# Shared blocks: the last products of a step are placed behind the first products of the next step

## The chip, the cores and the metric

The kernel runs on one core of one Trainium2 chip. The metric is the device time of one execution in microseconds. Three runs of the kernel before the change took 1549.39, 1553.00 and 1556.89 us; the median is 1553.0 us. The profile is of a further execution, and the sums below are made against that one.

## What is computed

The reference passes 2048 tokens of 256 channels (`x`, 2 x 1024 x 256, fp32) through four layers. Each layer adds to `x` what a conditioning stage followed by a mixture-of-experts stage makes of it. Cut to what this change touches:

```python
# layer 0, after its conditioning (32 routed experts, one per token)
shared = (silu(h @ shared_gate_w) * (h @ shared_up_w)) @ shared_down_w     # 256 -> 512 -> 256
x = x + shared + routed
# layer 2, conditioning: 2 shared experts of width 512, stacked to one of width 1024, and 8 routed, top 2
# layer 2, ffn: 8 shared experts of width 128, stacked to one of width 1024, and 8 routed, top 2
# layer 3, conditioning: one shared expert of width 512, and 8 routed, top 2
# layer 3, ffn: 16 experts with a capacity of 160 tokens each (no shared expert)
```

The shared part is the same computation in all four places: two products with the tokens, a silu and a multiplication, and a product back to 256 channels. Layer 1 has no shared expert.

## The kernel before

**The tiling.** Tokens are worked in four blocks of 512 (`TB`), the hidden width in pieces of 128. One call of `_shared` (L1347) does one block of tokens: it runs over `nf` pieces of the hidden width, 4 in layers 0 and 3 and 8 in the two stages of layer 2. One turn of that loop is called a step here. There are 16 steps in layer 0, 32 in the conditioning of layer 2, 32 in its ffn stage and 16 in layer 3: 96 steps.

**A step.** TensorE makes the first products `spg` and `spu` (L1360), each a sum over two halves of the 256 channels, in two PSUM tiles of the tag "mm", of which there are four. ScalarE makes `ssg = silu(spg)` (L1365), VectorE makes `sa = ssg * spu` (L1367), and TensorE makes the last products from `sa`: four matmuls (L1370), one for each 128 tokens of the block, which add into the two PSUM tiles `spo`. In the trace each of these fp32 matmuls has two records, so a step has four of `spg`, four of `spu` and eight of `spo`. After the last step of a block, VectorE or ScalarE adds or copies `spo` into the token-major arrays (L395, L1760, L1859). `ssg` and `sa` have two buffers each.

**What sets the order.** The program is written as a list, and a planner in the compiler orders each engine's queue from it at compile time: by the order in the list, by the dependences, and by its own estimate of when each input is ready. It may pull later work forward while an earlier instruction is not ready by that estimate. `_behind` (L1329) adds an edge that only fixes an order on one engine's queue; it makes nothing wait on a semaphore. On the chip each queue is worked in the order planned.

**What hangs on a step.** `_shared` takes two callbacks. `mid(f, mul, mm)` is called after the first products; `hook(f, mul, mm)` is called after the last products; `mul` is the multiplication of a step and `mm` the last matmul. Through them other work is spread over the steps:

- In the stages that lead (three blocks of tokens in each of the two conditioning stages and the layer 2 ffn stage), `Lead.hook` (L317) starts the routing at the 2nd and 4th step (1st and 3rd in layer 3), and then sends token rows to DRAM with `Rows.scatter` (L278), an indirect DMA from GpSimd: two for each step in layer 2, four in layer 3, each made to wait for that step's `mul`. The routed slots that follow load these rows (`xs<-xbuf`, L297, SyncE), and a load waits for all 32 sends.
- In the stages that close (the last block of tokens), `Tokens.hook` (L1468) is both `hook` and `mid`: it loads routed outputs (`yt<-tbuf`), adds them on VectorE behind `mul` (L1459), and transposes finished tokens on TensorE behind `mm` (`_back`, L1378). In layer 3 it also starts pieces of the last stage (`Last.at`, L1963).
- In layer 0, the first two blocks have no callback; the last two gather routed outputs (`Combine.hook`, L1408), and the loads of layer 1's weights wait for the first step's `mul` (L631).

In time, the program is: layer 0 with its first two blocks (53 to 103 us), its routed slots, its last two blocks (279 to 327 us), layer 1, and then for each of the three further stages a lead, the routed slots and a closing block; the layer 3 ffn stage ends it.

Of the kernel before, what the change touches and what calls it, by code (L numbers as in the profile page):

```python
# [19 lines left out]
P = 128  # L20
# [281 lines left out]
class Lead:  # L302
# [14 lines left out]
    def hook(self, f, mul, mm):  # L317
        self.n += 1
        if self.n in self.at:
            self.part()  # L320
            if not self.at:

                for _ in range(min(self.per, len(self.sends))):
                    self.sends.pop(0)()
        elif self.n > self.late:
            for _ in range(min(self.per, len(self.sends))):
                self.sends.pop(0)(mul)
# [56 lines left out]
def _layer0(k):  # L384
# [6 lines left out]
    def shared(tb, hook=None):  # L391
        po = _shared(k, pool, psum, HT, tb, *shw, hook)
        for i in range(2):
            t = tb * 4 + i * 2
            nc.vector.tensor_tensor(Xt[:, t:t + 2, :], po[i], Xt[:, t:t + 2, :], ALU.add)  # L395
# [933 lines left out]
def _behind(k, inst, ref):  # L1329

    k.tc.add_manual_dep(inst.ins, ref.ins.name,
                        mybir.DependencyInfo(mybir.DependencyClass.NoSync,
                                             mybir.DependencyReason.SCHED_ONLY))
# [13 lines left out]
def _shared(k, pool, psum, X, tb, W1, W3, W2, nf, hook=None, mid=None):  # L1347

    nc = k.nc
    cols = slice(tb * TB, (tb + 1) * TB)
    po = [psum.tile([P, 2, D], F32, name="spo%d" % i, tag="o", bufs=2) for i in range(2)]
    mul = None
    for f in range(nf):
        pg = psum.tile([P, TB], F32, name="spg", tag="mm")
        pu = psum.tile([P, TB], F32, name="spu", tag="mm")
        for ps, W in ((pg, W1), (pu, W3)):
            for c in range(2):
                mm = nc.tensor.matmul(ps, W[:, c, f * P:(f + 1) * P], X[:, c, cols],  # L1360
                                      start=c == 0, stop=c == 1)
        if mid:
            mid(f, mul, mm)
        sg = pool.tile([P, TB], F32, name="ssg", tag="sg")
        k.silu = nc.scalar.activation(sg, pg, AF.Silu)  # L1365
        a = pool.tile([P, TB], F32, name="sa")
        mul = nc.vector.tensor_mul(a, sg, pu)  # L1367
        for g in range(4):

            mm = nc.tensor.matmul(po[g // 2][:, g % 2, :], a[:, g * P:(g + 1) * P], W2[:, f, :],  # L1370
                                  start=f == 0 and g % 2 == 0, stop=f == nf - 1,
                                  skip_group_check=True)
        if hook:
            hook(f, mul, mm)
    return po


# [263 lines left out]
class Split:  # L1641
# [32 lines left out]
    def end(self, i, aT, cols):  # L1674
        n, nc = self.n, self.k.nc
        po = self.psum.tile([P, D], F32, name="fpo", tag="o", bufs=2)
        self.stage([nc.tensor.matmul(po[r, :], aT[:, f, r], w[2][:, f, :], start=f == 0,
                                     stop=f == n - 1, skip_group_check=True)
                    for f in range(n) for r, w in cols])
        y = self.pool.tile([P, D], F32, name="ys", bufs=4)  # L1680
        nc.scalar.copy(y, po)
        self.slots.put(i, y)
# [21 lines left out]
def _cond_moe(k, name, wr, bias, W1, W3, W2, nf, hold, R1, R2, gate_mult, final, lead, next=None):  # L1704
# [47 lines left out]
    def shared(tb, hook=None, mid=None, added=lambda: False):  # L1752
        po = _shared(k, pool, psum, XT, tb, W1, W3, W2, nf, hook, mid)
        for i in range(2):
            t = tb * 4 + i * 2
            if added():
                nc.vector.scalar_tensor_tensor(Ht[:, t:t + 2, :], po[i], final, Ht[:, t:t + 2, :],
                                               ALU.mult, ALU.add)
            else:
                nc.scalar.activation(Ht[:, t:t + 2, :], po[i], AF.Copy, scale=final)  # L1760
# [51 lines left out]
def _layer2_ffn(k):  # L1812
# [42 lines left out]
    def shared(tb, hook=None, mid=None):  # L1855
        po = _shared(k, pool, psum, HT, tb, *shw, hook, mid)
        for i in range(2):
            t = tb * 4 + i * 2
            nc.vector.scalar_tensor_tensor(Xt[:, t:t + 2, :], po[i], 1.0 / 16.0, Xt[:, t:t + 2, :],  # L1859
                                           ALU.mult, ALU.add)  # L1860
# [510 lines left out]
```

## Time and profile before

| | |
|---|---|
| runs before, median of 3 (lowest to highest) | 1553.0 us (1549.39 to 1556.89) |
| the profiled execution | 1554.72 us |
| its span, first to last instruction | 1553.0 us, so 1.7 us lie around it |
| mean granted TensorE clock | 0.977 |
| TensorE busy / VectorE / ScalarE / GpSimd | 95% / 31% / 20% / 18% |
| first products, L1360, four groups | 102.1 + 97.5 + 91.6 + 90.4 us busy |
| last products, L1370 | 192.5 us busy in 768 records |
| DMA | 252.43 MB in packets, 163 GB/s mean |

A matmul's busy time runs to its modelled end, and matmuls overlap: a 512-column matmul of `spg` has a mean of about 600 ns though the next one follows 430 ns later. So the distance between starts says what a matmul costs in a full queue, and the busy column doesn't. "PEld" is the weight load, which overlaps the matmul before it. "Idle before" is time in which the engine had nothing running ahead of an instruction of the group, with what ended it.

### The profile page before, as it was taken

What the parts mean: (1) busy time and instruction counts of PE and PEld (TensorE: products, weight loads), DVE (VectorE), ACT (ScalarE), POOL (GpSimd) and SP (SyncE); (2) the same over time, 40 slices, a digit from 0 to 9 for tenths busy, and PEclk for the clock granted to TensorE, in tenths of its full rate; (3) what the DMA queues carried; (4) which work ended last, traced back from release to release, by engine and by line L of the source; (5) the groups of instructions that cost most, each with busy time, mean ns of one, the idle gap of its engine ahead of it and who ended that gap; (6) DMA issues with size and microseconds to landing.
All of it is one profiled execution on the core that took longest, in us unless ns stands there. A gap on an engine that the chain in (4) does not pass through costs nothing. (4 is left out here: it accounts for less than half of the span.)

```text
span 1553.0 us, 23694 instructions
## 1 busy us (share of the span) xinstructions
PE 1470.2 (95%) x8649; PEld 1021.0 (66%) x8652; DVE 478.2 (31%) x1596; ACT 303.9 (20%) x642; POOL 285.2 (18%) x317
## 2 busy tenths in 40 slices
PE   6989999999999999999999999999999989998897
PEld 2543333444555886555699999999985547864675
DVE  3732222324411444421111111111114414446432
ACT  2311212123111212211111111111111212126222
POOL 0400000300331441033001001010010253420342
PEclk9989999999999999999999999999999999999799
DMA  9859995923211684051053254155517437762470
GB/s 253 273 201 332 337 352 175 255 72 123 96 48 35 195 252 136 0 214 52 28 185 116 94 190 174 36 184 184 180 34 263 139 122 246 214 218 83 146 250 19
DMA packets 184239, 252.43 MB, mean 163 GB/s; under 512 B 17111, under 2 KB 137823, under 8 KB 184112
## 3 DMA queue, kind: packets, MB, share of 16 engines
q1 hardware_dynamic: 164448, 210.92, 42.2%
q0 software_dynamic: 14176, 36.63, 6.6%
q10 hardware_dynamic: 5488, 3.25, 0.7%
q8 instruction: 72, 1.18, 0.3%
q14 instruction: 55, 0.45, 0.1%
HBM read 284.86 MB, written 50.76 MB: 216 GB/s over the span
## 5 line engine op out<-in xcount | busy, mean ns | idle before, releaser
L1370 PE MATMUL spo<-ring,sa 128*128 128x256 f32 x768 | 192.5, 393 | 20.2 <-DVE sa L1367 15.1
L1370 PEld LDWEIGHTS spo<-ring,sa 128*128 128x128 f32 x768 | 140.7, 192 | 101.9 <-DVE sa L1367 71.5
L281 POOL DMA_INDIRECT tbuf<-ys,sdst x114 | 112.1, 984 | 509.4 <-ACT ys L1635 381.9
L1367 DVE TENSOR_TENSOR sa<-ssg,spu 128x512 f32<-128x512 f32 x96 | 65.8, 686 | 327.3 <-PE spu L1360 287.3
L1628 DVE TENSOR_TENSOR fa<-fsg,fpu 128x512 f32<-128x512 f32 x72 | 49.5, 687 | 316.0 <-PE fpu L1623 316.0
L1623 PE MATMUL fpu<-xsT,ring 128*128 128x128 f32 x1152 | 140.4, 275 | 0.0
L1623 PE MATMUL fpg<-xsT,ring 128*128 128x128 f32 x1152 | 140.3, 275 | 0.0
L1623 PEld LDWEIGHTS fpg<-xsT,ring 128*128 128x128 f32 x1152 | 137.1, 192 | 1.9
L1623 PEld LDWEIGHTS fpu<-xsT,ring 128*128 128x128 f32 x1152 | 134.4, 192 | 0.0
L1632 PE MATMUL fpo<-ring,fa 128*128 128x256 f32 x576 | 130.3, 379 | 0.0
L1365 ACT ACTIVATE ssg<-spg 128x512 f32<-128x512 f32 x96 | 57.3, 597 | 347.7 <-PE spg L1360 217.5
L1632 PEld LDWEIGHTS fpo<-ring,fa 128*128 128x128 f32 x576 | 106.7, 190 | 13.0
L1360 PE MATMUL spg<-HT,ring 128*128 128x512 f32 x192 | 102.1, 621 | 5.4 <-issue 2.8
L1360 PE MATMUL spg<-XT,ring 128*128 128x512 f32 x192 | 97.5, 599 | 0.1
L1360 PE MATMUL spu<-HT,ring 128*128 128x512 f32 x192 | 91.6, 596 | 0.0
L1360 PE MATMUL spu<-XT,ring 128*128 128x512 f32 x192 | 90.4, 592 | 0.0
L1599 PE MATMUL cph<-xsT,ring 128*128 128x128 f32 x624 | 83.9, 277 | 6.7 <-DMA ring<-in_L_r 3.7
L1599 PEld LDWEIGHTS cph<-xsT,ring 128*128 128x128 f32 x624 | 76.0, 192 | 10.4 <-DVE sn L1527 4.8
L1606 PE MATMUL cpo<-ring,ch 128*128 128x256 f32 x312 | 80.1, 380 | 0.8 <-ACT ch L1602 0.8
L1627 ACT ACTIVATE fsg<-fpg 128x512 f32<-128x512 f32 x72 | 43.0, 597 | 169.7 <-PE fpg L1623 169.7
L1360 PEld LDWEIGHTS spu<-XT,ring 128*128 128x128 f32 x192 | 36.6, 191 | 43.8 <-issue 43.6
L1360 PEld LDWEIGHTS spu<-HT,ring 128*128 128x128 f32 x192 | 36.6, 194 | 41.9 <-issue 41.7
(574 smaller groups left out, 1656.5 us busy)
## 6 DMA issues: line engine op xcount, KB each, us to landing
ring<-in_L_w SPq DMA_DIRECT2D x108, 1024.0 KB
ring<-in_L_r SPq DMA_DIRECT2D x96, 512.0 KB
ring<-in_L_r SPq DMA_DIRECT2D x156, 256.0 KB
xs<-xbuf SPq DMA_DIRECT2D x138, 129.0 KB
ring<-in_L_W SPq DMA_DIRECT2D x32, 512.0 KB
yt<-tbuf SPq DMA_DIRECT2D x48, 256.0 KB
xbuf<-ACC SPq DMA_DIRECT2D x1, 6063.0 KB
ring<-in_L_s SPq DMA_DIRECT2D x6, 512.0 KB
```

Source lines behind the costliest of these rows:

```text
L281: i = k.nc.gpsimd.indirect_dma_start(out=self.ap, out_offset=bass.IndirectOffsetOnAxis(ap=idx, axis=0), in_=rows, in_offset=None, **end)
L1360: mm = nc.tensor.matmul(ps, W[:, c, f * P:(f + 1) * P], X[:, c, cols], start=c == 0, stop=c == 1)
L1365: k.silu = nc.scalar.activation(sg, pg, AF.Silu)
L1367: mul = nc.vector.tensor_mul(a, sg, pu)
L1370: mm = nc.tensor.matmul(po[g // 2][:, g % 2, :], a[:, g * P:(g + 1) * P], W2[:, f, :], start=f == 0 and g % 2 == 0, stop=f == nf - 1, skip ...
L1599: made = [nc.tensor.matmul(ph[:, f, :], R1[:, c, f * P:(f + 1) * P], xT[:, c, :], start=c == 0, stop=c == 1) for f in range(2) for c in ra ...
L1606: made = [nc.tensor.matmul(po, h[:, f, :], R2[:, f, :], start=f == 0, stop=f == 1) for f in range(2)]
L1623: made = [nc.tensor.matmul(ps[:, j, :], W[:, c, (f0 + j) * P:(f0 + j + 1) * P], xT[:, c, :], start=c == 0, stop=c == 1) for ps, W in ((pg, ...
L1627: nc.scalar.activation(sg, pg, AF.Silu)
L1628: nc.vector.tensor_mul(a[:, f0:f0 + 4, :], sg, pu)
L1632: made = [nc.tensor.matmul(po, a[:, f, :], W2[:, f, :], start=f == 0, stop=f == 4 * nh - 1) for f in range(4 * nh)]
```

## The change

The last products of a step are no longer written after its multiplication. They are kept as a function `end`, and written one step later, after the first products of the next step, with an order edge behind the last of these (`mm`, the last matmul of `spu`). The callback `hook` moves with them, and is called with the old step's `f` and `mul`, and the last matmul of its last products. The last step of a block has no next one: its last products are written at the end without an edge. `mid` stays where it was. No computation, tile, buffer or transfer is added or removed.

```diff
+    def end(f, a, mul, ref):
+        for g in range(4):
+            mm = nc.tensor.matmul(po[g // 2][:, g % 2, :], a[:, g * P:(g + 1) * P], W2[:, f, :],
+                                  start=f == 0 and g % 2 == 0, stop=f == nf - 1,
+                                  skip_group_check=True)
+            if ref is not None:
+                _behind(k, mm, ref)
+        if hook:
+            hook(f, mul, mm)
+
+    old = None
     for f in range(nf):
...
         sg = pool.tile([P, TB], F32, name="ssg", tag="sg")
         k.silu = nc.scalar.activation(sg, pg, AF.Silu)
+        if old:
+            end(*old, mm)
         a = pool.tile([P, TB], F32, name="sa")
         mul = nc.vector.tensor_mul(a, sg, pu)
-        for g in range(4):
-
-            mm = nc.tensor.matmul(po[g // 2][:, g % 2, :], a[:, g * P:(g + 1) * P], W2[:, f, :],
-                                  start=f == 0 and g % 2 == 0, stop=f == nf - 1,
-                                  skip_group_check=True)
-        if hook:
-            hook(f, mul, mm)
+        old = f, a, mul
+    end(*old, None)
     return po
```

## Prediction

> **What bounds the kernel now.** I read the page first: the busy row of TensorE, and the groups of a step.
>
> ```profile
> PE 1470.2 (95%) x8649; PEld 1021.0 (66%) x8652; DVE 478.2 (31%) x1596; ACT 303.9 (20%) x642; POOL 285.2 (18%) x317
> L1370 PE MATMUL spo<-ring,sa 128*128 128x256 f32 x768 | 192.5, 393 | 20.2 <-DVE sa L1367 15.1
> L1370 PEld LDWEIGHTS spo<-ring,sa 128*128 128x128 f32 x768 | 140.7, 192 | 101.9 <-DVE sa L1367 71.5
> ```
>
> TensorE is the bound. The one wait that recurs on it is for `sa` before the last products. How much it costs depends on the row. The first says 20.2 us idle before L1370. The Trainium skill (Perfetto Trace Analysis, section Identifying the Most-Contended Engine) says that matmul busy time is a poor measure of headroom, since pipelined matmuls hide it. So I went to the timeline of one regular step of the layer 2 lead, engine by engine (start, duration, engine, line).
>
> ```profile
> 425.97 0.19 PEld L1360 LDWEIGHTS spg<-XT,ring 128*128 128x128 f32 x1 [0.24 <-issue]
> 426.40 0.19 PEld L1360 LDWEIGHTS spg<-XT,ring 128*128 128x128 f32 x1 [0.24 <-issue]
> 427.41 1.59 PEld L1370 LDWEIGHTS spo<-ring,sa 128*128 128x128 f32 x8 [0.82 <-DVE sa L1367]
> ...
> 426.40 1.02 PE L1360 MATMUL spg<-XT,ring 128*128 128x512 f32 x2
> 427.41 1.99 PE L1370 MATMUL spo<-ring,sa 128*128 128x256 f32 x8
> 429.24 0.59 PE L1360 MATMUL spg<-XT,ring 128*128 128x512 f32 x1
> ...
> 426.67 0.69 DVE L1367 TENSOR_TENSOR sa<-ssg,spu 128x512 f32<-128x512 f32 x1 [4.73 <-PE spu L1360]
> ```
>
> The planner already pulls half of the next `spg` (two records at 426.40) ahead of the last products. That covers 0.86 us of the roughly 1.3 us from the last `spu` to the end of `sa`, not all. First products start 0.43 us apart (425.97, 426.40), so the last products could start at 426.40 + 2 x 0.43 = 427.26; they start at 427.41, when `sa` is done: **0.15 us**. Their first weight load has waited too, so the eight take 427.41 to 429.24 = 1.83 us. Where `sa` is early they take less:
>
> ```profile
> 619.65 1.89 PE L1370 MATMUL spo<-ring,sa 128*128 128x256 f32 x8
> 621.38 1.02 PE L1360 MATMUL spg<-XT,ring 128*128 128x512 f32 x2
> ```
>
> That is 1.73 us, so **0.10 us** more. A full step without waiting is 8 x 0.43 + 1.73 = 5.16 us; the regular one has 5.42 us (427.41 to 432.83). The loss is 0.26 us a step, although the rows above show a TensorE that is "busy" throughout.
>
> I made this subtraction from the start times of all 96 steps. Regular stalls of 0.26 us: 55 steps, 14.2 us. All stalls, by stage: layer 0's first blocks 7.7, its last blocks 5.3, layer 2 conditioning lead 6.6 and close 0.8, ffn lead 7.3 and close 1.0, layer 3 lead 10.8 and close 3.4: **43 us**. By the idle column it would be 20. I take the starts.
>
> **What the change does to it, part by part.** The order becomes g1 u1 o0 g2 u2 o1 (g, u first products, o last products). Between u and its own o now stand the whole g and u of the next step, 3.43 us, instead of 0.86: 2.57 us more cover. Instructions, semaphores and bytes are unchanged; the edge waits for nothing. ScalarE and VectorE keep their work. Banks: u of step f+1 needs the "mm" tile that `sa` of f-1 frees, some 7 us before; `sa` of f+1 needs the buffer that o of f-1 reads, which stands ahead of g and u of f+1. So no new wait there in a regular step. At the end of a block o of the last step now has o of the step before as cover (1.73 us).
>
> - Regular stalls: all go, 14.2 us.
> - Layer 0, first blocks, 7.7 us. One step waits 4.2 us for `sa`, which VectorE had queued behind a comparison of the mask that waits for its load. 4.2 - 2.57 = 1.6 us stays, and 1.6 us of the first two steps isn't a wait for `sa`. Gain 4.5.
> - Layer 0, last blocks, 5.3 us: stalls of 1.5, 1.4 and 1.0 us, where `sa` stands behind gathered rows on VectorE. All under 2.57, so all go. Gain 5.3.
> - Layer 2: 6.6 + 7.3 in the leads (the longest is 1.1 us, behind the routing's burst on VectorE), 0.8 + 1.0 in the closes. Their scatters go out two a step and end some four steps before the lead does, so the slots start with TensorE. Gain 15.7.
> - Layer 3, lead, 10.8 us. Here something else is late next. The scatters:
>
> ```profile
> 1231.86 1.13 POOL L281 DMA_INDIRECT xbuf<-Xt,l3c_rows  x1 [72.36 <-DVE l3c_rows_w L250]
> 1279.17 0.96 POOL L281 DMA_INDIRECT xbuf<-Xt,l3c_rows  x1 [0.30 <-issue]
> 1282.83 1.86 SPq L297 DMA_DIRECT2D xs<-xbuf  x4
> 1286.26 0.41 DVE L1523 COPY xsT<-ps_cm 128x256 f32<-128x256 f32 x1
> 1287.83 1.05 PE L1599 MATMUL cph<-xsT,ring 128*128 128x128 f32 x8
> ```
>
> First scatter 1231.86, last 1279.17, row loads 1282.83, transposed rows 1286.67, first slot 1287.83. The slack is only 1.1 us. In between, GpSimd needs 32 x (0.96 + 0.30) = 40.3 us of the 48.3 from first start to last end: 8 us are its waits for late `sa`. Now the routing is moved as well: `hook` comes one step later, so the logits wait for o0 behind g1 and u1. They began 5.9 us after the stage did; now 2 x 3.43 + 1.73 = 8.6. Its second part stood in the list behind o2, and was pulled ahead of it while `sa` was late; now o2 is ready, and g3 u3 stand in front. I take 3.6 us later in all. GpSimd then runs nearly unbroken, and its end comes 8.0 - 3.6 = 4.4 us earlier; with the slack, 5.5 us at best of the 10.8. TensorE is done some 6 us before the rows are there.
>  That gap is where a rule speaks against the change. The window table (us, busy times, then PEclk, DMA share, GB/s) has:
>
> ```profile
> 86.50:92.30 5.80, 5.80 (x11) 3.87 (x12) 2.34 (x3) 0.28 (x1) 0.00 (x0) 0.50 1.08 372
> ```
>
> After the 4.2 us stall of layer 0 the clock was 0.50 for 5.8 us, a loss of 2.9. The Trainium skill (TensorE: Matmul & The Clock Gate, HAM oscillation) says that an idle window of 3.4 us halves the clock, until a busy one releases it: 1.7 us by the rule for one window, 2.9 by the row. I take the row for the new gap: 5.5 - 2.5 = gain **3**; bounds -3 (the routing slips two steps) and +10.8 (nothing is late).
> - Layer 3, close, 3.4 us. The chain of waits runs there through VectorE and the `yt` loads, not only TensorE:
>
> ```profile
> 1399.08 7.00 DMA yt<-tbuf
> ```
>
> These loads wait for buffers that additions behind `sa` of the last step free. That `sa` comes earlier (u3 no longer stands behind o2), but the loads' own 7 us remain. Half: gain 2; bounds -2 (a piece of the last stage is called behind u3 instead of o2) and +5.
> - Clock in layer 0: the 4.2 us stall becomes 1.6, perhaps with no slow window (0 to 1.3 us beyond what is counted). Taken as 0.
>
> Sum: 4.5 + 5.3 + 15.7 + 3 + 2 = **30.5 us**. Against the profiled execution: 1554.7 - 30.5 = **1524 us**; it stands 1.7 us above the median of the runs, well inside their spread of 7.5. Nothing else takes the time back: the routed slots start when their stage ends, and in them TensorE waits little for weights (3.7 us in all for `ring`, in the list of waits).
>
> **Rivals.**
>
> A, *all of it*: the scatters don't hold layer 3. For it: 8 us of their waits vanish. Against it: 40.3 us of GpSimd work with 1.1 us of slack. 1554.7 - 43 = 1512.
>
> B, *only the regular stalls*: the longer stalls sit in the in-order queue of VectorE, and a new plan may put a burst ahead of `sa` again, or a DMA ends the stage. 1554.7 - 14.2 = 1541.
>
> C, *hidden anyway*: the stages end on transfers and GpSimd, whose items fill the page's chain of waits in layer 3. Then about 1553. Against it: in layer 2 the scatters end four steps early.
>
> D, *slower: the queue's head is blocked*. Now o of f-1 is pinned behind g and u of f. If those can't start, a ready o stands behind them. The place is the routing: its logits and counts take tiles of the tag "mm". The row totals `l2f_R` are written at 657.13 and read at 660.01, so a bank is held for about 3 us, and the top-two burst on VectorE is 4.2 us (648.2 to 652.4). If g or u of the next step is given such a bank, TensorE stops for up to 3.1 + 4.2 us at each of three routings, 22 us, with two slow windows of 2.9 about 28. It decides when a bank is held past the 3.4 us that the pinned work covers, and when the gain is rival B's: 1554.7 - 14.2 + 28 = 1569. Against it: before the change these tiles rotate in the same banks, and only 1.1 us was lost.
>
> **How the numbers follow.** Forecast 0.60, A 0.10, B 0.15, C 0.07, D 0.08. The forecast's own range is 1514 to 1537 by the bounds of layer 3 and of the first blocks. To leave out no more than 0.2 the range takes in A and B: 1508 to 1545. A measurement of this kernel can tell about 0.5%, 7.8 us, from no change: faster is forecast, A and B, 0.85; C is same, 0.07; D slower, 0.08.
>
> **What would show it.** In the profile after: steps 5.16 us apart in the layer 2 leads; eight L1370 records in 1.89 us everywhere, with hardly any idle time before them from `sa`; VectorE's `sa` ending over 2 us before they start. First layer 3 scatter 25 to 28 us after the stage starts, then scatters 1.26 us apart with few breaks, and TensorE idle before the first layer 3 slot with PEclk near 0.5 after it. A gap before `spg` or `spu` in a routing would speak for D. I am wrong if the steps stay at 5.42, if the leads are shorter but the slots no earlier, or if new waits of more than 15 us stand before L1360.

## The result and the profile after

Four runs of the changed kernel took 1524.94 to 1529.91 us, median 1529.36; the kernel before, run beside it, 1554.95 us (1549.39 to 1557.90). The ratio is 0.9835, interval 0.9812 to 0.9858: 1.65% faster. The profiled execution is at 1529.61 us (span 1527.9), 25.1 us under that of before; the forecast was 30.5 us under.

The page of the changed kernel, busy row and the groups of the last products (their line is now L1360, `ssg` is L1379, `sa` L1383):

```profile
PE 1448.0 (95%) x8648; PEld 1025.1 (67%) x8652; DVE 479.2 (31%) x1596; ACT 304.8 (20%) x642; POOL 287.4 (19%) x317
L1360 PE MATMUL spo<-ring,sa 128*128 128x256 f32 x768 | 182.3, 383 | 13.8 <-DVE sa L1383 13.8
L1360 PEld LDWEIGHTS spo<-ring,sa 128*128 128x128 f32 x768 | 145.5, 191 | 63.9 <-issue 31.5
```

The weight loads waited 71.5 us for `sa` before; now that wait isn't what the idle column names. TensorE's idle time before L1360 went from 20.2 to 13.8 us, and those 13.8 us are nearly one wait, of 12.9 us, which this document is mostly about.

A regular step, timeline of the changed kernel in the layer 2 lead (start, duration, engine; PE is TensorE, ACT ScalarE, DVE VectorE, and further on POOL is GpSimd and SPq SyncE's queue of transfers):

```profile
424.12 0.60 ACT L1379 ACTIVATE ssg<-spg 128x512 f32<-128x512 f32 x1 [4.56 <-PE spg L1374]
425.63 1.89 PE L1360 MATMUL spo<-ring,sa 128*128 128x256 f32 x8
425.91 0.69 DVE L1383 TENSOR_TENSOR sa<-ssg,spu 128x512 f32<-128x512 f32 x1 [4.47 <-PE spu L1374]
427.36 1.88 PE L1374 MATMUL spg<-XT,ring 128*128 128x512 f32 x4
429.08 1.88 PE L1374 MATMUL spu<-XT,ring 128*128 128x512 f32 x4
430.80 1.46 PE L1360 MATMUL spo<-ring,sa 128*128 128x256 f32 x6
```

The last products started at 425.63 use the `sa` of the step before. The `sa` of 425.91 ends at 426.60 and is needed at 430.80, 4.2 us later. (The last row counts six records because the view ends there.) From start to start the step takes 430.80 - 425.63, in unrounded times 5.16 us; the eight records take 427.36 - 425.63 = 1.73 us.

By stage, each from its first matmul to that of the next (us; the gains are from unrounded times; the forecast is the prediction's own gain for the same stretch):

| stage | before | after | gain | forecast |
|---|---|---|---|---|
| layer 0, first blocks | 63.3 | 55.9 | 7.4 | 4.5 |
| layer 0, last blocks | 53.5 | 48.1 | 5.4 | 5.3 |
| layer 2, conditioning lead | 136.6 | 129.6 | 7.0 | 6.6 |
| layer 2, conditioning close and ffn lead | 182.0 | 173.8 | 8.1 | 0.8 + 7.3 |
| layer 2, ffn close, and layer 3 lead | 127.3 | 129.2 | **-1.8** | 1.0 + 3 |
| layer 3, close and routing of the last stage | 83.9 | 84.9 | **-1.1** | 2 |
| all others (slots, layer 1, last stage, start), -1.9 to 1.8 each | | | 0.1 | 0 |

The first four rows gave 27.9 us where 24.5 were forecast. The two rows with layer 3 in them gave -2.9 where 6 were.

In layer 0's first blocks no stall is left. The window table of the changed kernel (us, busy times of PE, PEld, DVE, ACT, POOL, then PEclk, DMA share, GB/s):

```profile
86.00:92.00 6.00, 6.00 (x19) 3.42 (x18) 0.69 (x1) 0.60 (x1) 0.10 (x1) 1.00 0.99 352
```

Where before stood a wait of 4.2 us and then 5.8 us at a clock of 0.50, the clock is 1.00. The reason isn't on TensorE. VectorE's `sa` stood behind a comparison (`l_ne`, L667) of the mask's last quarter, and that waited for its load. SyncE's queue, before and then after:

```profile
79.67 0.34 SPq L297 DMA_DIRECT2D xs<-xbuf  x1
80.12 0.38 SPq L665 DMA_DIRECT2D l_mm<-in_mask  x1
```

```profile
70.05 0.37 SPq L665 DMA_DIRECT2D l_mm<-in_mask  x1
84.20 0.34 SPq L297 DMA_DIRECT2D xs<-xbuf  x1
```

The load stood behind the first load of routed rows, which has to wait for the scatters; the new plan has it ahead, 10 us earlier. The comparison starts at 80.24 us instead of 83.56, and delays no `sa` that is needed.

The layer 3 lead is another matter. Timeline of the changed kernel:

```profile
1207.70 1.04 POOL L281 DMA_INDIRECT xbuf<-Xt,l3c_rows  x1 [74.56 <-DVE l3c_ef L238]
...
1219.27 1.88 PE L1374 MATMUL spg<-XT,ring 128*128 128x512 f32 x4
...
1231.81 0.96 POOL L281 DMA_INDIRECT xbuf<-Xt,l3c_rows  x1 [0.30 <-issue]
1236.15 0.60 ACT L1379 ACTIVATE ssg<-spg 128x512 f32<-128x512 f32 x1 [19.53 <-remote]
1236.78 0.69 DVE L1383 TENSOR_TENSOR sa<-ssg,spu 128x512 f32<-128x512 f32 x1 [17.52 <-ACT ssg L1379]
1237.53 3.78 PE L1360 MATMUL spo<-ring,sa 128*128 128x256 f32 x8 [12.94 <-DVE sa L1383]
1237.75 0.96 POOL L281 DMA_INDIRECT xbuf<-Xt,l3c_rows  x1 [4.98 <-DVE sa L1383]
```

Read from the bottom: TensorE waits 12.9 us for an `sa`, VectorE for `ssg`, and ScalarE does that `ssg` at 1236.15, although the records of its `spg` end at 1221.15. ScalarE had nothing else to do. Meanwhile GpSimd sent scatters 1.265 us apart without a break, the last of them at 1231.81, and then waited for the same `sa`. In the same stretch SyncE works through a chain of small instructions that read the slots' expert numbers (L1506); 17 instructions of SyncE in this lead take about 0.70 us each, where those of the chain later take 0.28 us or less.

"remote" means that a semaphore released the instruction, but that no instruction of the profile ended just then. The trace also keeps the times at which semaphores were updated, which the views don't print. Of TensorE, VectorE and ScalarE none is recorded between 1209.69 and 1236.13. Then three of TensorE's stand at 1236.13, 1236.17 and 1236.21, for records of `spg` and `spu` that ended at 1221.15 to 1222.86, and `ssg` starts 0.02 us after the first. This points to a ScalarE that was ready and waited for TensorE's signal. Some updates of that stretch are missing from the trace (10 of the 16 due from TensorE between the first scatter and the last are there), so it can't be said from them alone that the signal itself was late and not only its record. A late start of this kind is called a hold below.

The stage with the lead in it, as a sum of three parts, makes the loss plain (us from the trace, each part rounded; the last column is the stage in the table above):

| kernel | stage start to first scatter | first scatter to end of last | end of last to first slot | sum |
|---|---|---|---|---|
| before | 71.4 | 48.3 | 7.7 | 127.3 |
| after | 73.6 | 48.0 | 7.6 | 129.2 |

The scatters start later and take as long as before. That TensorE's own steps became shorter doesn't appear in the sum.

### The profile page after: what moved, and what is told of

Its sections match the earlier page's. It is cut to its first block, busy times and chain, and to the rows that moved or that the text cites. A ratio compares the mean times of both kernels' runs of the same rounds, so it can differ in the third digit from the quotient of the medians.

```text
span 1527.9 us, 23703 instructions
## 1 busy us (share of the span) xinstructions
PE 1448.0 (95%) x8648; PEld 1025.1 (67%) x8652; DVE 479.2 (31%) x1596; ACT 304.8 (20%) x642; POOL 287.4 (19%) x317
## 5 line engine op out<-in xcount | busy, mean ns | idle before, releaser
L1360 PE MATMUL spo<-ring,sa 128*128 128x256 f32 x768 | 182.3, 383 | 13.8 <-DVE sa L1383 13.8
L1360 PEld LDWEIGHTS spo<-ring,sa 128*128 128x128 f32 x768 | 145.5, 191 | 63.9 <-issue 31.5
L1383 DVE TENSOR_TENSOR sa<-ssg,spu 128x512 f32<-128x512 f32 x96 | 65.8, 686 | 290.6 <-PE spu L1374 230.2
L1379 ACT ACTIVATE ssg<-spg 128x512 f32<-128x512 f32 x96 | 57.3, 597 | 329.7 <-PE spg L1374 274.0
L1374 PE MATMUL spg<-HT,ring 128*128 128x512 f32 x192 | 95.1, 611 | 5.6 <-issue 2.9
L1374 PE MATMUL spg<-XT,ring 128*128 128x512 f32 x192 | 90.6, 593 | 0.1
```

## The experiments

Two theories were open for the 12.9 us: GpSimd's unbroken train of scatters holds ScalarE, VectorE and SyncE (an engine is held when it starts long after the records of its inputs end); or SyncE's chain of loads does. Beside them: is it the edge or the place in the list that works, what did the later hook cost, and how much cover is needed. The kernel before took 1553.75 us beside e1 to e4, 1554.77 beside e5 to e8, 1545.94 beside e9 and e10 and 1543.71 beside e11 and e12, on four different chips; so times are compared by their ratio, with its 95% interval. In the texts of this part a wait of TensorE is counted by starts, as in the prediction; the idle column prints about 0.15 us less. An `ssg` is late from the last start of its `spg` plus 0.43 us, and one that isn't held comes 0.2 us after that.

**e1_no_edge.** The list order of the change, without the edge.

```diff
-            end(*old, mm)
+            end(*old, None)
```

> The last products stay written one step later, without the edge behind the first products. Theory 'place in the list': the planner keeps them there by itself wherever sa is ready by its estimate, so steps stay 5.16 us apart in the layer 2 leads, and the time is that of the change, 1529 us, within 5. Rival 'the edge': without it the planner pulls the last products ahead of the second half of the next first products, steps go back to 5.3 to 5.4 us, and the time is 1540 to 1550 us.

1527.33 us, ratio 0.9838 (0.9803 to 0.9872). All stages are within 1.1 us of the changed kernel's, but for layer 0's slots, 2.4 us longer, and the close of layer 2 with the layer 3 lead, 2.4 us shorter. The place in the list does it, and the edge isn't needed for it. Whether those two stages differ by the edge was not tried.

**e2_hook_stays.** The callback is called at its old place, at the end of its own step.

```diff
-        if hook:
-            hook(f, mul, mm)
...
         mul = nc.vector.tensor_mul(a, sg, pu)
+        if hook:
+            hook(f, mul, mm)
```

> The last products move as in the change, but hook is called where it was before (with the last matmul of spu as mm). Theory: the call one step later is what delays the first scatter of layer 3 from 23.1 to 26.9 us after the stage starts, and what costs the layer 3 close about 1 us; here the first scatter comes at 23 to 24 us, the close gains 1 to 3 us, and the time is 1523 to 1528 us. Rival: the routing's own chain sets the first scatter, it stays at 26 to 27 us, and the time stays at 1529.

1525.63 us, ratio 0.9825 (0.9797 to 0.9853). The first scatter comes 66.7 us after the stage starts, not 73.6: the later hook cost 6.9 us, and pinning alone gains 4.7 on before. The stage with the layer 3 lead is 123.4 us, 5.7 less than after, and the layer 3 close 1.7 less. But `ssg` is still late, by up to 9.2 us, and TensorE waits 3.7 and 1.9 us for `sa` and 3.5 us for rows. Layer 0 and layer 2 keep their gains.

**e3_three.** Three scatters for each step of layer 3 instead of four.

```diff
-    lead_ = Lead(k, routing, *((2, 4), 2) if nf == 8 else ((1, 3), 4))
+    lead_ = Lead(k, routing, *((2, 4), 2) if nf == 8 else ((1, 3), 3))
```

> The change, with three scatters a step instead of four in the layer 3 lead, so that GpSimd pauses for over 1 us in each step. Theory GpSimd: ScalarE and VectorE are held back while GpSimd sends scatters one after another, and are let go in its pauses; then the 13 us wait for sa in this lead is gone (under 2 us), SyncE's 0.7 us instructions become fewer, and though the last scatter is sent later in the step order the slots begin no later than in the change; 1520 to 1530 us. Theory SyncE: its chain of slot-number loads is what holds them; a wait of 5 to 13 us for sa stays, and the slots begin 5 us or more later; 1533 to 1540 us.

1528.43 us, ratio 0.9841 (0.9813 to 0.9869). One `ssg` is 10.8 us late, and TensorE waits 8.7 us for its `sa`. Three a step gives no break at first: the routing ends late, so the first 17 scatters go out in one train (1205.78 to 1227.03), and the hold falls into it. From then on GpSimd breaks after every few, and no `ssg` is late; but the train ends later (50.9 us from first to last), and the slots wait 7.4 us for rows. A poor test of the breaks, as it turned out.

**e4_eid_late.** SyncE reads the numbers of slots 4 and later from a copy that VectorE makes only after the last `sa` of the lead, so that SyncE is quiet while the scatters go out.

```diff
...
+        eid2 = rp.tile([1, NS], I32, name=name + "_eid2")
+        _behind(k, nc.vector.tensor_copy(eid2, eid), k.mul)
...
-        slots.slot(i, _gelu_products(k, pool, psum), lambda: _slot_weights(k, eid, i, sets, E))
+        slots.slot(i, _gelu_products(k, pool, psum),
+                   lambda: _slot_weights(k, eid if i < 4 else eid2, i, sets, E))
```

> The change, with the slot numbers for layer 3's slots 4 to 38 copied by VectorE behind the last sa of the lead, so that SyncE's chain of loads runs after the scatters and not beside them. Theory SyncE: the 13 us wait for sa is gone, GpSimd sends its 32 scatters in about 41 us, the slots begin 5 to 8 us earlier; 1521 to 1525 us, if the late loads don't hold up the slots. Theory GpSimd: a wait of 5 us or more for sa stays; 1529 us or later.

1531.35 us, ratio 0.9867 (0.9839 to 0.9895). Only 4 slow instructions of SyncE are left in the lead, and still `ssg` is up to 6.7 us late and TensorE waits 5.8 and 3.0 us. So a hold doesn't need SyncE's chain. The hold is shorter than in the changed kernel, though, where `ssg` is 15.2 us late, and the stage is 124.5 us, 4.7 less than after; that the chain lengthens a hold isn't excluded. The time isn't better because the slots, with their numbers late, take 5.5 us more than before.

**e5_half.** The last products stand behind the next `spg` alone, 1.72 us of cover instead of 3.44.

```diff
             for c in range(2):
                 mm = nc.tensor.matmul(ps, W[:, c, f * P:(f + 1) * P], X[:, c, cols], ...)
+            if ps is pg and old:
+                end(*old, mm)
...
-        if old:
-            end(*old, mm)
```

> The last products are pinned behind the first half of the next step's first products only (its spg, 1.72 us), not behind all of them (3.44 us). Theory 'any cover does': the regular step needs only 0.26 us of cover, so steps of 5.16 us as in the changed kernel; of the long waits 1.72 us less is hidden at each of the few places (first steps of a block, the steps around routing, the held step in the layer 3 lead): at most 5 such places, so a time 0 to 6 us above the changed kernel, 1529 to 1535. Rival 'full cover is needed': sa often comes later than 1.72 us after the last spu, regular steps stay at 5.3 to 5.4 us, and the time is near that of before, above 1540.

1538.28 us, ratio 0.9903 (0.9868 to 0.9938): 3 us outside what was expected. Regular steps do take 5.16 us, and the layer 2 rows gain 6.0 and 6.4 us. The layer 0 blocks gain only 2.2 and 1.6 where the changed kernel gains 7.4 and 5.4. The lines that tell why in the first blocks, from SyncE's queue and TensorE's timeline in this kernel:

```profile
80.65 0.34 SPq L297 DMA_DIRECT2D xs<-xbuf  x1
81.09 1.70 SPq L665 DMA_DIRECT2D l_mm<-in_mask  x1
```

```profile
88.18 2.81 PE L1360 MATMUL spo<-ring,sa 128*128 128x256 f32 x8 [3.94 <-DVE sa L1383]
```

Here the plan keeps the mask's load behind the routed rows, as before the change, and the wait stays nearly whole: 3.94 us in the idle column, and 4.03 before. The plan of before already had 0.86 us of cover at this place, so only 0.86 is new here, and the comparison, whose load went out in 1.70 us and not 0.38, starts 4.6 us after the last products of the step before and not 3.8. In the last blocks stalls of 0.8, 1.5 and 1.0 us stay, which full cover hides. For the regular stall half the cover is enough.

**e6_one_scatter.** The plainest test of the hold. The changed kernel, with 31 of 32 scatters of layer 3 left out.

```diff
         lead_.sends = k.x.paced(k.Xr, rows)
+        if nf == 4:
+            lead_.sends = lead_.sends[-1:]
```

> The changed kernel with 31 of the 32 scatters of layer 3's routing left out (the slots of layer 3 then read rows of an earlier layer); the slot-number loads of SyncE and everything else stay. Theory 'GpSimd's unbroken train holds the others': no ssg or sa of the layer 3 lead comes more than 1 us late, the 13.1 us stall before spo is gone, SyncE's loads of slot numbers take about 0.26 us each and not 0.70, and the stage 'layer 2 close and layer 3 lead' is 10 to 20 us shorter than in the changed kernel. Rival 'SyncE's chain of loads holds them': the loads still take 0.70 us, and a hold of over 5 us stays.

1507.95 us in one run. No `ssg` is late by more than 0.2 us, none of SyncE's loads takes 0.70 us, and the stage is 113.6 us, 15.5 less than after. From its timeline, where the changed kernel stood still:

```profile
1215.92 0.60 ACT L1379 ACTIVATE ssg<-spg 128x512 f32<-128x512 f32 x1 [4.56 <-PE spg L1374]
1221.09 0.60 ACT L1379 ACTIVATE ssg<-spg 128x512 f32<-128x512 f32 x1 [4.56 <-PE spg L1374]
1225.39 0.60 ACT L1773 ACTIVATE ACC<-spo 128x512 f32<-128x512 f32 x1 [3.71 <-PE spo L1360]
```

SyncE's chain is all there, and holds nobody. So the scatters are needed for the hold, and SyncE's slowness goes with them too. With the 31 instructions of GpSimd their transfers are gone as well; which of the two is needed isn't shown.

**e7_trains8** and **e8_trains11.** The hook at its old place, and the 32 scatters in trains with breaks between them. For e8, cut (for e7: 4, 4, 8, 8, 8 at steps 3, 4, 6, 9, 11):

```diff
+    def train(self, mul):
+        n, ref = self.plan.get(self.n, (0, None))
+        for _ in range(n):
+            self.sends.pop(0)({'mul': mul, 'silu': self.k.silu}.get(ref))
...
+    if nf == 4:
+        lead_.plan = {3: (4, None), 4: (6, "mul"), 7: (11, "silu"), 10: (11, "silu")}
```

> The hook at its old place, and the 32 scatters of layer 3 sent as four trains of 8 with breaks of 2 to 3 us between them (each train waits for an sa or ssg of a later step). In the runs so far the first late ssg came 13 to 14 us after a train began, that is after some 11 scatters. Theory 'a train longer than 11 scatters holds the others': no ssg or sa more than 1 us late, scatters end at about 1250, TensorE waits only for xs, 6 to 9 us, at the end of the lead; time 1522 to 1527. Rival 'the hold has to do with the number of scatters or loads since the routing, not with an unbroken train': ssg or sa late by more than 3 us in spite of the breaks; time 1527 to 1535.

> As with trains of 8, but trains of 10, 11 and 11 with breaks of about 1.6 us. Theory 'a train longer than 11 scatters holds the others, a short break lets go': late by at most 2 us, scatters end at about 1246.5, TensorE waits about 4 us for xs; time 1519 to 1524, the fastest so far. Rival 'a break of 1.6 us is too short' or 'the number since the routing counts': an ssg or sa late by more than 3 us, time 1525 to 1532.

e7: 1522.72 us, ratio 0.9794 (0.9757 to 0.9830). e8: 1520.56 us, ratio 0.9783 (0.9745 to 0.9822). Both times are as the first theory had them, but neither is free of holds: the latest `ssg` comes 4.5 us late in e7 (9.2 in e2) and 5.6 us in e8, and TensorE waits 4.0 us in e7 and 1.8 and 2.9 us in e8. In e7 the late one falls in a train of 8 that came after a break of 1.2 us. So "longer than 11 scatters" isn't the rule, and the two rivals that count since the routing aren't excluded.

**e9_before_trains** and **e10_trains7.** The same trains in the kernel before, and trains of 7 with the hook at its old place.

```diff
+        lead_.plan = {3: (4, None), 4: (3, "mul"), 6: (7, "mul"), 8: (7, "mul"), 10: (7, "mul"), 12: (4, "silu")}
```

> The kernel before (last products right after their own sa), and only the 32 scatters of layer 3 sent as trains of 10, 11 and 11 with breaks. It asks what the trains are worth without the pinned products. Theory 'two separate costs': the holds of before (waits of 3.7, 0.8 and 2.9 us before spo in the layer 3 lead) shrink to 3 us in all, but the scatters must still end before layer 3 starts, so the lead shortens by 2 to 5 us; time 1548 to 1553. Rival 'the trains do nearly all that the best kernel gains on the changed one': the lead shortens by 8 us or more, time under 1547.

> As the trains of 11 with the hook at its old place, but trains of 7, 7, 7, 7 and 4 with breaks of about 1 to 1.5 us. Theory 'shorter trains are held less': waits of TensorE for a late sa under 2 us in all in the layer 3 lead, scatters end at about 1246, time 1518 to 1521. Rival 'the length of a break decides, and these are too short': an sa or ssg late by over 3 us as in the trains of 8, time 1521 to 1526.

e9: 1553.16 us, ratio 1.0055 (1.0021 to 1.0089), slightly slower than before; neither of its theories had that. e10: 1517.52 us, ratio 0.9824 (0.9791 to 0.9857). In both not one `ssg` is late. In e9 that buys nothing (list of waits in the layer 3 lead):

```profile
PE ps_cm L369 <- DMA xs<-xbuf: 6.5, 2, 6.2
PE spo L1380 <- DVE sa L1377: 0.4, 1, 0.4
```

The waits for `sa` have gone, and a wait of 6.2 us for the rows stands in their place; the stage is 126.9 us against 127.3. The breaks of e9 keep its train nearly as long as the holds did, 46.6 us against 48.3. What ends the lead, before the change too, is the last scatter and what follows it.

**e11_unbroken.** Whether the hold lasts as long as the train: no scatter of layer 3 waits for an `sa`. **e12_trains7_again** is e10 once more.

```diff
-                self.sends.pop(0)(mul)
+                self.sends.pop(0)(mul if self.per == 2 else None)
```

> The hook at its old place, and no scatter of layer 3 waits for an sa: GpSimd sends all 32 without a break, in 32 times 1.265 or 40.4 us, 5.1 us less than the train takes with the waits. Theory 'the hold lasts as long as the train': from some 14 us after the first scatter ScalarE and VectorE are held until 1 to 4 us after the last one, about 28 us; TensorE has work for one step beyond and waits 15 to 25 us, and the layer 3 lead is 5 to 15 us longer than with the hook at its old place and the waits kept (123.4 us). Rival 'the hold ends by itself, the pauses that followed it were chance': the longest wait of TensorE for an sa is under 8 us, and the lead is 118 to 123 us, since the scatters end at about 1243.

> The trains of 7 once more, for a better ratio to the kernel before: 0.977 to 0.982, which would put it below the changed kernel's 0.9835.

e11 took 1520.32 us in one run, and neither theory foresaw it. All 32 scatters go out in 40.25 us without a break, and nobody is held. Timeline of e11, 35 us into the train:

```profile
1235.07 0.96 POOL L281 DMA_INDIRECT xbuf<-Xt,l3c_rows  x1 [0.30 <-issue]
1235.15 0.60 ACT L1377 ACTIVATE ssg<-spg 128x512 f32<-128x512 f32 x1 [4.56 <-PE spg L1372]
1236.33 0.96 POOL L281 DMA_INDIRECT xbuf<-Xt,l3c_rows  x1 [0.30 <-issue]
1236.67 1.89 PE L1360 MATMUL spo<-ring,sa 128*128 128x256 f32 x8
1236.94 0.69 DVE L1381 TENSOR_TENSOR sa<-ssg,spu 128x512 f32<-128x512 f32 x1 [4.47 <-PE spu L1372]
```

So a second condition is needed. On the chips of e9 to e12 no profile shows a late `ssg`, whatever the train (1 or 2 slow instructions of SyncE in the lead). On the chips of e1 to e8 every kernel with the 32 scatters has one (13 to 21 slow ones, but for e4, which had moved them), as have the profiles of before and after. No kernel was profiled on both kinds of chip, so the lead alone can't tell the chip from the kernel. A stage that no edit touches can: in the slots of layer 2's conditioning, where GpSimd also sends scatters, some 305 semaphore updates of TensorE, VectorE and ScalarE are due. The traces of before, after and e1 to e8 have 190 to 221 of them (e6, which has no hold, 202), those of e9 to e12 303 to 306. In the stage with the layer 3 lead e6 has all its updates too, and each held kernel lacks 11 to 29. So the condition goes with the chip, or with something that was at work beside the kernel there, and the scatters bring it out. Every time on record here comes with the profiler's span and clock, so it isn't shown either that the hold is there without the profiler.

The kernel before is 8 to 11 us faster on the chips without the hold. Its steps in this lead are 5.42 us apart where nothing is held (e9) and four scatters take 5.06, so by estimate its train would last 40 to 43 us without holds, 5 to 8 less than 48.3; its trace from such a chip wasn't taken, so that is a fit and not shown. It would also explain why e9's breaks, 46.6 us from first scatter to last, lose there.

e11's stage is 113.7 us, 13.7 less than before and as short as that of e6, which sends one scatter. Yet the kernel gains little by it: the slots after it take 94.6 us, not 83.9. Its queue of transfers on SyncE, and its list of waits:

```profile
1242.86 1.77 SPq L297 DMA_DIRECT2D xs<-xbuf  x4
1253.23 4.50 SPq L2102 DMA_DIRECT2D XT<-in_L_b  x9
1257.84 0.84 SPq L297 DMA_DIRECT2D xs<-xbuf  x2
```

```profile
PE ps_cm L359 <- DMA xs<-xbuf: 11.2, 1, 11.2
```

Nine loads of `XT` for a later stage stand between the row loads of slots 4 and 5. They aren't issued until 1253.23, and the rows behind them wait: TensorE stands 11.2 us. In e10 these nine went out before the first row load. e11 with them in front wasn't run.

e12: 1519.86 us, ratio 0.9838 (0.9818 to 0.9859). The expectation (0.977 to 0.982) failed. Its stage is 120.1 us. The parts of the stage in these kernels:

| kernel | to first scatter | first to last scatter | to first slot | sum | late `ssg` |
|---|---|---|---|---|---|
| e2, hook at its old place | 66.7 | 45.6 | 11.1 | 123.4 | 9.2 us |
| e8, trains of 11 | 66.5 | 46.1 | 7.4 | 120.0 | 5.6 us |
| e9, before with trains | 71.4 | 46.6 | 8.9 | 126.9 | none |
| e10, trains of 7 | 66.5 | 45.5 | 6.1 | 118.2 | none |
| e11, unbroken | 68.2 | 40.2 | 5.2 | 113.7 | none |

Whether any version beats the changed kernel is open. The trains have ratios of 0.978 and 0.979 where the hold appears, and 0.982 and 0.984 where it doesn't; the changed kernel has 0.9835, and wasn't run beside them on one chip.

## Why the prediction was right, and where not

The sum, 25.1 us for 30.5, is nearer than its parts: layer 0 gave 3.0 us more than forecast, most of it by luck, and layer 3 8.9 less.

**The bound and the regular stalls: right.** Steps of 5.16 us and records of 1.89 us, as forecast. In layer 2 the leads and the conditioning close gave 15.1 us for the 14.7 forecast. e5 confirms the size of the term: 1.72 us of cover is enough for it.

**Layer 0, first blocks: forecast 4.5, measured 7.4, by another way.** The step took the wait of 4.2 us less 2.57 us of new cover, "1.6 us stays". Nothing stayed, and the clock never fell, since the load that VectorE waited for was planned ahead of another in SyncE's queue. That was luck: nothing in the forecast pointed to it. In e5, where that load kept its place, 0.86 us more cover took 0.1 us off the wait, as the comparison came 0.8 us later as well. The prediction looked at the queues of TensorE and VectorE here, and not at SyncE's, which the planner orders anew as well.

**Layer 0, last blocks: right,** 5.4 for 5.3.

**Layer 3, lead: the failed step.** Forecast 3, measured -2.8 (the row's -1.8, less 1.0 for the ffn close, if that came as forecast). The step's parts: the first scatter was put 3.6 us later, that is 26.8 us after the matmuls of the lead begin behind the close's last products (1231.86 - 1208.66 = 23.2 before), and came at 1207.70 - 1180.44 = 27.3. Right to half a microsecond. Then "GpSimd then runs nearly unbroken, and its end comes 8.0 - 3.6 = 4.4 us earlier". The 8.0 us of its waits for late `sa` did not go: 48.0 us from first to last against 48.3. The prediction took these `sa` as late because of TensorE's order, which the change mends. They were late mainly since ScalarE and VectorE were held while GpSimd sent (e6: the changed kernel without the scatters has none late). The changed order doesn't end such a hold. The profile of before had the sign of it, an `sa` with "remote" as its releaser:

```profile
1247.68 0.69 DVE L1367 TENSOR_TENSOR sa<-ssg,spu 128x512 f32<-128x512 f32 x1 [8.32 <-remote]
```

So of the 10.8 us of stalls in that lead none was won by moving the last products. The stalls themselves weren't what made the lead long: in e9 they are gone, the train of scatters is nearly as long, and so is the lead. That GpSimd runs unbroken, and the lead becomes shorter, once nothing is held and no scatter waits for an `sa`, is what e11 shows on another chip: 40.2 us of scatters, and a stage of 113.7 us. The hook's place was counted at 3.6 us from the lead's first matmul; by e2 it is worth 6.9 us of the stretch to the first scatter, since pinning alone would have brought that 4.7 us forward.

**The slow clock after the new wait: over-sized.** 2.5 us were set aside, near the 2.9 of the row; the rule that was weighed against it gave 1.7, an estimate from the page's window of 3.4 us. Window table of the changed kernel:

```profile
1230.00:1237.53 7.53, 0.01 (x1) 0.01 (x1) 0.69 (x1) 0.60 (x1) 2.16 (x3) 0.50 0.15 53
1237.53:1241.00 3.47, 3.47 (x8) 2.84 (x9) 0.00 (x0) 0.60 (x1) 2.64 (x3) 0.50 0.21 76
1241.00:1246.00 5.00, 5.00 (x13) 2.28 (x13) 0.69 (x1) 1.20 (x2) 1.35 (x3) 0.98 0.15 53
```

After the wait 3.47 us ran at 0.50, half of it lost: 1.7 us. Here the rule of the Trainium skill (TensorE: Matmul & The Clock Gate, sections What's actually happening and HAM oscillation), one slow window after an idle stretch, was the better guide; the 5.80 us at 0.50 that the row of before shows are longer than one window. The gap that it was forecast for, ahead of the first layer 3 slot, didn't come: the 12.9 us stood earlier, and TensorE arrived as late as the rows.

**Layer 3, close: wrong sign.** Forecast 2 (bounds -2 and 5), measured -1.1. The last products did end earlier: 22.8 us after the last output scatter, not 25.5, and the last stage's first routing product (`l3f_ps`) came at 26.5, not 29.4. But the last transposition of finished tokens came at 35.5, not 36.2, and the comparisons of that routing (`l3f_d`) began at 35.2, not 32.4; its last product came 1.1 us later than before. With the hook at its old place (e2) it came 0.6 us earlier than before. That fits the lower bound's reason, "a piece of the last stage is called behind u3 instead of o2". That it is this piece, and not another thing in the hook, wasn't tried.

**The rivals.** B and C fall, as layer 0 and layer 2 gave all that was there. A falls at layer 3. D falls: no gap stands before `spg` or `spu` at a routing, and the largest new wait there is 0.57 us, before `spo`. In the changed kernel the queue's head was blocked, but by `sa` and at the scatters.

## What to carry to other kernels

Placing a consumer one step later in the program, behind the next step's producers, removes a recurring short wait that the busy column hides; half the cover does that here, and the rest pays only at longer stalls. What hangs on the moved piece, callbacks above all, is worth trying at its old place: here that brought the first scatter 6.9 us forward and the stage 5.7 us down, though the two kernels' ratios, 0.9825 and 0.9835, don't tell them apart. Before a stall is booked as a gain, read what released it and what ends the stage: a wait on "remote", or one beside a chain of GpSimd and transfers that ends as late, isn't sure to be mended by reordering TensorE.

## What was not expected of the hardware

On some chips ScalarE and VectorE started up to 15 us after the records of their inputs had ended, while GpSimd sent indirect DMAs 1.265 us apart, and small instructions of SyncE took 0.70 us each. They went on 0.7 to 4 us after GpSimd paused, though in e4, e5, e7 and e8 a late one also went on inside a train. Where this happens the trace shows the inputs' semaphore updates late: the first late `ssg` of the changed kernel and of e1 to e4 starts 0.02 to 0.03 us after an update with which a gap of 10 to 26 us in the records ends. Without the scatters it doesn't happen (e6). On two other chips it didn't happen, even with 32 scatters in a row on one of them (e11). What the second condition is, and why the updates come late, stays open. The same kernel before differed by 0.7% between these chips (1543.71 and 1545.94 against 1553.75 to 1554.95).
